# Three places of a four-layer graph network: result places behind the gate, more store buffers and numbers by GpSimd, attention's weights loaded at the far end of memory

## The chip, the cores and the metric

The kernel runs on one core of a Trainium2 chip. A core has a matrix engine (TensorE; PE in the profile, its weight loads PEld), a vector engine (VectorE, DVE), a scalar engine (ScalarE, ACT), GpSimd (POOL) and SyncE (SP). Each engine works through a queue of its own in a fixed order; they wait for each other by semaphores. Transfers are issued from the queues of SP, ACT and POOL (SPq, ACTq, POOLq where a profile speaks of the queue itself) and run on 16 DMA engines that all of them share. The metric is the device time of one execution, in microseconds.

## What is computed

The network takes 2708 nodes of 256 features and a 2708 x 2708 adjacency matrix, and runs four layers, each a graph attention and a feed-forward part, all float32. The change touches what follows the second graph layer's start: the first mixture (feed-forward part of layer 1), the attention and the second mixture (feed-forward part of layer 2). Cut to those:

```python
x = x + L1_gnn(layernorm(x), adj)
# first mixture: each node is computed by its best of 8 experts
H = gelu(layernorm(x) @ W1 + b1, approximate=False)        # 1024 wide
probs = softmax(H @ Wg + bg); assign = argmax(probs)
for e in range(8):
    out = out + where(assign == e, probs[:, e] * (H @ Wd[e] + bd[e]), 0)
x = x + out
x = x + L2_gnn(layernorm(x), adj)
# second mixture, after causal self-attention
h = rmsnorm(layernorm(x), ln1_w)
q, k, v = h @ wq.T, h @ wk.T, h @ wv.T                      # rotated, causal softmax
xa = layernorm(x) + attention(q, k, v) @ wo.T
flat = rmsnorm(xa, ln2_w)
weights = top 2 of softmax(flat @ router_w.T), made to sum to 1
for e in range(8):
    hh = silu(flat @ w1[e].T) * (flat @ w3[e].T)            # 682 wide
    out = out + weights[:, e] * (hh @ w2[e].T)
x = x + xa + out
```

## The kernel before

Nodes lie on 128 partitions, in 22 tiles of rows. A recording layer traces the program, plans the order of each engine's queue and sets the semaphores; a block `with tc.issue_after(i)` puts the instructions of it behind `i`, but only those on the engine of `i`. A buffer comes from a pool (`bufs` of them under one name), and whoever takes it waits for its last users. A pool lies at the left or, with `side="right"`, at the right end of on-chip memory; when a pool is closed its place is given to later ones, which then wait for all that used it.

**Dispatch by sorting.** `Routing` gives each choice of a node a slot in its expert's region of a DRAM table (`hs`; for the first mixture a table `fnodes` of node numbers alone). Slots are worked off in tiles of 128: the first eight tiles are the first of each expert, the others belong to an expert that is known only at run time. The usual count of such tiles is 26 in the first mixture and 47 in the second; any beyond them stand in a conditional block (`others`).

**First mixture** (`top1_ffn`). Blocks of 512 nodes go through `hidden` (L943 matmuls, gelu), `gate`, and `store`, which transposes the hidden rows back (L960), copies them out (L961, by ACT for the `late` ones) and stores them by SP in DRAM (`hidden`, L964). The last two blocks are stored after all matmuls: the first of them, eight copies, into free rooms of buffers that are no longer used (`spare`, two tiles called ft and one called ht512); the second, four copies, into `hr`, three buffers. Then the numbers of the nodes are read back: `load_first` (L1629) reads 8 rows of 128 numbers by SP, 18 more loads of one row each follow on SP (L1625), TensorE turns the 8 rows (L1049), VectorE casts them (L1050), and POOL gathers the hidden rows by them, four tiles ahead (L1061, `hr<-hidden,number`). Tiles are then transposed (L1074) and multiplied (L1110), and POOL scatters the results to DRAM (L1648).

**Second graph layer** (`gat_single`). For each of four blocks of up to 768 nodes, and each of 22 source tiles j, ACT makes e (L674), VectorE masks it (L675), TensorE accumulates (L1310). At i0 = 0, j = 3 VectorE also copies the bias (`late`, L1304), and POOL adds it to X (L1307), 22 instructions. `Weights` loads w2 at the right end by SP (L1380, L1381) behind a memset of POOL (L1378).

**Attention.** The pool `a_w` holds ln1, wv, wk and wq. It lies at the left end, where the graph layer's buffers were. POOL loads the four (L1735 and the helper `load_weight`, L93), VectorE scales the three matrices by ln1 (L1739, two instructions each), and `project(0)` normalises four tiles (f, L108), transposes them (L1759) and multiplies (pv, sc). When the last projection is done, `proj.close()` frees `a_w`, and w1 of the experts is loaded at the right end.

**Second mixture** (`experts`). For each tile s: SP loads f from `hs`, four tiles ahead, into five buffers (`fetch`); `front` transposes f (L116) and ACT copies it (ft, L1972); `hidden` multiplies by w1 and w3; ACT applies silu (L2003); `gate` multiplies the two on VectorE (L2007); `transposes` turns the result (L2014), VectorE and ACT copy it (ht, L2015 and L2016); `results` multiplies by w2 (po, L2022), ACT copies (L2026) and POOL scatters to `dys` (L1648). `place` computes, from the two last columns of f, where the result goes: three small VectorE instructions in `where` (L1638, L1641, L1642). TensorE's order is written out by hand: hidden, transposes of the tile before, hidden, results, front of the next tile but one, hidden, hidden.

Of the kernel before, what the change touches and what calls it, by code (L numbers as in the profile page):

```python
# [8 lines left out]
F32 = mybir.dt.float32  # L9
# [3 lines left out]
ALU = mybir.AluOpType  # L13
# [3 lines left out]
P = 128  # L17
# [646 lines left out]
def gat_pairs(net, e, j, i0, iw, big_p, ratio):  # L664

    nc = net.nc
    v = e[:, :iw]
    i = slice(i0, i0 + iw)
    nc.scalar.activation(v, big_p[:, i], AF.Relu, bias=net.minus_one, scale=ratio)  # L674
    return nc.vector.scalar_tensor_tensor(v, v, 1.0, net.mask[:, j, i], ALU.add, ALU.mult)  # L675
# [201 lines left out]
def top1_ffn(net, ctx):  # L877
# [4 lines left out]
    nc, tc, a, X = net.nc, net.tc, net.a, net.X  # L882
    E, HID = 8, 1024
    KC = HID // P
    with ExitStack() as inner:
# [21 lines left out]
        with tc.tile_pool(name="f1tp", bufs=2, space=PSUM) as ptp, tc.tile_pool(  # L907
            name="f1h", bufs=2, space=PSUM
        ) as ph, tc.tile_pool(name="f1g", bufs=1, space=PSUM) as pg, tc.tile_pool(
            name="f1r", bufs=2  # L910
# [38 lines left out]

            def store(its, halves, late=False, room=()):  # L950


                room = list(room)
                for k, t in enumerate(its):
                    r = rows(t)
                    for n, half in enumerate(halves):
                        hr = room.pop(0) if room else rp.tile([P, 512], F32, name="hr", bufs=3)
                        ps = pg.tile([P, 4, P], F32, name=f"hr{n}")
                        for c in range(KC // 2):
                            nc.tensor.transpose(ps[:r, c, :], half[:, c, k * P : k * P + r], net.ident)  # L960
                        (nc.scalar.copy if n or late else nc.vector.tensor_copy)(  # L961
                            hr[:r], ps[:r].rearrange("p c m -> p (c m)")
                        )
                        last = nc.sync.dma_start(rows_of[span(t), n * 512 : (n + 1) * 512], hr[:r])  # L964
                return last
# [51 lines left out]

            spare = [work.tile([P, 2, 512], F32, name="spare", tag="ft") for _ in range(2)]
            spare.append(work.tile([P, KC // 2, 512], F32, name="spare", tag="ht512", bufs=3))
            room = [t[:, k, :] for t in spare for k in range(t.shape[1])]  # L1020
            for k in kept:
                store(*k, True, room)
                room = ()
        route.finish()
        prep = ctx.enter_context(tc.tile_pool(name="g2prep", bufs=1))
        with tc.tile_pool(name="f1t", bufs=1, space=PSUM) as pt, tc.tile_pool(
# [10 lines left out]
            def load(group, at):  # L1037
                node = rowed[at : at + len(group), :]
                if group[0] == 0:
                    route.load_first(node)  # L1040
                else:
                    for k, s in enumerate(group):
                        route.load(s, node[k : k + 1, :])
# [120 lines left out]
def gat_single(net, key, head, feed, elu):  # L1164
# [7 lines left out]
    with ExitStack() as ctx:  # L1172
# [121 lines left out]
        for i0, iw in chunks(W):  # L1294
            its = tiles_of(i0, iw)
            acc = [pacc.tile([P, D + 1], F32, name="acc") for _ in its]
            for j in range(NT):
                e = work.tile([P, W], F32, name="e")
                masked = gat_pairs(net, e, j, i0, iw, big_p, ratio[:, j : j + 1])
                if bias is not None and i0 == 0 and j == 3:  # L1300

                    late = small.tile([P, D], F32, name="late", bufs=1)
                    with tc.issue_after(masked.ins):
                        nc.vector.tensor_copy(late, bias)  # L1304
                    for t in range(NT):
                        r = rows(t)
                        nc.gpsimd.tensor_tensor(X[:r, t, :], X[:r, t, :], late[:r], ALU.add)  # L1307
                for k, i in enumerate(its):
                    ri = rows(i)
                    nc.tensor.matmul(  # L1310
                        acc[k][:ri], e[:, k * P : k * P + ri], V[:, j, :], start=j == 0, stop=j == NT - 1
                    )
            for k, i in enumerate(its):
                r = rows(i)
                rd = small.tile([P, 1], F32, name="rd")
                nc.vector.reciprocal(rd[:r], acc[k][:r, D : D + 1])
                if not elu:
                    nc.vector.scalar_tensor_tensor(
                        X[:r, i, :], acc[k][:r, :D], rd[:r], X[:r, i, :], ALU.mult, ALU.add
                    )  # L1320
                    continue

                h = work.tile([P, D], F32, name="h", bufs=6)
                nc.scalar.activation(h[:r], acc[k][:r, :D], AF.Copy, scale=rd[:r])
                g = work.tile([P, D], F32, name="g")
                nc.vector.tensor_scalar(g[:r], h[:r], 0.0, None, ALU.min)
                nc.scalar.activation(g[:r], g[:r], AF.Exp)
                nc.vector.tensor_scalar(h[:r], h[:r], 0.0, -1.0, ALU.max, ALU.add)
                nc.vector.tensor_tensor(g[:r], g[:r], h[:r], ALU.add)
                nc.vector.tensor_tensor(X[:r, i, :], X[:r, i, :], g[:r], ALU.add)  # L1330
# [65 lines left out]
class Routing:  # L1396
# [216 lines left out]
    def load(self, s, f):  # L1613

        sync = self.net.nc.sync
        if s < self.E:
            self.loaded = sync.dma_start(f, self.hs[s * CAP : s * CAP + P, :])
            return

        with nullcontext() if s == self.usual else self.net.tc.issue_after(self.loaded.ins):  # L1620
            row = sync.value_load(
                self.row[0:1, s : s + 1], min_val=0, max_val=(self.E - 1) * CAP + (NT - 1) * P
            )
        rows_of = self.hs[bass.ds(row, P), :]
        self.loaded = sync.dma_start(f, rows_of.rearrange("p d -> d p") if self.choices == 1 else rows_of)  # L1625

    def load_first(self, f):

        self.loaded = self.net.nc.sync.dma_start(  # L1629
            f, self.hs.rearrange("(e c) d -> e (c d)", e=self.E)[:, :P]  # L1630
        )

    def where(self, work, s, f):

# [56 lines left out]
def attention(net, route, ln2, router, weights):  # L1691
# [11 lines left out]
    with ExitStack() as ctx:  # L1703
# [25 lines left out]
        make_upper_triangular(nc, upper)  # L1729

        proj = core.enter_context(ExitStack())
        wp = proj.enter_context(tc.tile_pool(name="a_w", bufs=1))
        pp = proj.enter_context(tc.tile_pool(name="a_p", bufs=2))
        ln1 = wp.tile([P, 2], F32, name="ln1")
        nc.gpsimd.dma_start(ln1, a["d_ln1"].rearrange("(c p) -> p c", p=P))  # L1735
        wv, wk, wq = (net.load_weight(wp, a[f"d_w{n}T"], f"w{n}") for n in "vkq")
        for w in (wv, wk, wq):
            for c in range(2):
                nc.vector.tensor_scalar(w[:, c, :], w[:, c, :], ln1[:, c : c + 1], None, ALU.mult)  # L1739
        queries, results = {}, {}  # L1740

        def project(n):
# [208 lines left out]
def experts(net, route, weights, shares):  # L1951

    nc, tc = net.nc, net.tc
    E, HID, KC, KP = weights.E, weights.HID, weights.KC, weights.KP
    HALF = HID // 2
    with ExitStack() as ctx:
# [17 lines left out]
        def place(s):  # L1974
            tos[s] = route.where(work, s, fs.pop(s))
# [28 lines left out]

        def gate(s):
            h2 = hhs[s][:, :HID].rearrange("p (q m) -> p q m", q=2)
            nc.vector.tensor_tensor(h2, h2, halves.pop((s, 1))[:, :, :HALF], ALU.mult)  # L2007

        def transposes(s):
            hh = hhs.pop(s)  # L2010
# [19 lines left out]
        def through(s0, s1):  # L2030


            for s in range(s0, min(s0 + 4, s1)):
                fetch(s)
            front(s0)
            number(s0, nullcontext())
            number(s0 + 1, nullcontext())
            for q in range(2):
                last = hidden(s0, 0, q)
            silu(s0)  # L2040
            front(s0 + 1)
            for q in range(2):
                last = hidden(s0, 1, q)
            gate(s0)
            if s0 == 0:
                route.owners()
            place(s0)
            place(s0 + 1)
            if s0 == 0:
                shares()  # L2050
            for s in range(s0, s1):
                if s + 1 == s1:
                    results(s, transposes(s))
                    break
                with tc.issue_after(last.ins):
                    last = hidden(s + 1, 0, 0)
                with tc.issue_after(last.ins):
                    ht = transposes(s)
                last = hidden(s + 1, 0, 1)
                silu(s + 1)  # L2060
                with tc.issue_after(last.ins):
                    last = results(s, ht)
                if s + 4 < s1:
                    fetch(s + 4)
                if s + 2 < s1:
                    with tc.issue_after(last.ins):
                        front(s + 2)
                        place(s + 2)
                with tc.issue_after(last.ins):
                    last = hidden(s + 1, 1, 0)  # L2070
                if s + 2 < s1:
                    number(s + 2, tc.issue_after(last.ins))
                with tc.issue_after(last.ins):
                    last = hidden(s + 1, 1, 1)
                gate(s + 1)

        through(0, route.usual)
        with route.others():
# [192 lines left out]
```

## Time and profile before

| | |
|---|---|
| runs shown | 2853.90, 2859.36, 2853.67 us; median 2853.9 |
| the profiled execution's own time | 2853.26 us |
| its span | 2851.6 us |
| mean granted TensorE clock | 0.955 |
| TensorE busy | 2625.3 us, 92% of the span |
| VectorE, ScalarE, GpSimd busy | 51%, 36%, 13% |
| first mixture, hidden layer to last scatter | about 1075 to 1344 us |
| second graph layer, matmuls L1310 | 1399.5 to 1616.0 us |
| attention | 1616 to 2126 us |
| second mixture | about 2132 to 2530 us |

A line of the costliest groups reads: source line, engine, operation, output<-inputs, partitions x elements, xcount | busy us, mean ns of one | idle us of the engine just before them, and the releaser that ended most of it. In the chain that ended last each line is start, duration, and engine, tile and line of the work; "DMA f<-hs" is a transfer that the chain waited for, "issue" is time for which the profile shows no reason. A timeline line is start, duration (of the merged group), engine, line, operation, output<-inputs, and in brackets the idle time before it and what ended that.

### The profile page before, as it was taken

Reading aid. Unit: us, or ns where it says so; the run is one execution under the profiler, and the core shown is the slowest. Engines: PE = TensorE matmul, PEld = TensorE weight load, DVE = VectorE, ACT = ScalarE, POOL = GpSimd, SP = SyncE. Lnnn points to the kernel's source line nnn. Section 1 sums busy time; section 2 is a strip of 40 time slices with the busy share of each in tenths; the row PEclk is TensorE's granted clock in tenths of the full one; section 3 lists DMA queues with packets and bytes.
Section 4 is the critical chain, followed back from the end, with each engine's and each line's share of the span. In section 5 each row is a group of like instructions: output and inputs, shape, how many; then the busy total and the mean of one; then the engine's idle time right before and its main releaser. Section 6 shows DMA issues by size and latency. Waiting matters only on the chain.

```text
span 2851.6 us, 32365 instructions
## 1 busy us (share of the span) xinstructions
PE 2625.3 (92%) x11712; PEld 1616.6 (57%) x11712; DVE 1446.4 (51%) x3086; ACT 1040.0 (36%) x1639; POOL 381.5 (13%) x470
## 2 busy tenths in 40 slices
PE   5999989799999999888999899999969999969998
PEld 4667746563333444577788533333337777757885
DVE  7753348453777765422544456464653222245555
ACT  3344433224665653311543223233322221225453
POOL 1000012100000001143300123223331111110002
PEclk9999999797999999989999999899979999989999
DMA  8899210000000003753200100002031111041001
GB/s 295 288 299 326 97 65 1 3 5 1 1 1 1 1 3 115 169 176 128 85 1 1 34 23 18 16 0 94 16 117 32 30 30 34 28 137 62 1 1 40
DMA packets 107336, 197.67 MB, mean 69 GB/s; under 512 B 8831, under 2 KB 64361, under 8 KB 104341
## 3 DMA queue, kind: packets, MB, share of 16 engines
q1 hardware_dynamic: 89178, 147.89, 16.4%
q0 software_dynamic: 14624, 43.22, 4.6%
q10 hardware_dynamic: 3374, 4.46, 0.5%
q8 instruction: 98, 1.61, 0.2%
q14 instruction: 62, 0.50, 0.1%
HBM read 135.82 MB, written 59.71 MB: 69 GB/s over the span
## 4 chain that ended last, share of the span: by engine, by line
PE 74%; DVE 9%; issue 5%; DMA 5%; ACT 3%; POOL 3%; another core or an unknown queue 0%; ACTq 0%; SPq 0%; POOLq 0%; DVEq 0%
PE acc L1310 15%; PE acc L805 8%; PE acc L284 7%; PE den L816 4%; PE po L2022 4%; PE po L1836 3%; PE sc L1817 3%; PE score L273 3%; PE pv L123 3%; PE h L1990 3%; DMA f<-hs 2%; PE h L943 2%; PE po L123 2%; PE sc L1785 2%; PE pl L123 1%
## 5 line engine op out<-in xcount | busy, mean ns | idle before, releaser
L675 DVE SCALAR_TENSOR_TENSOR e<-e,mask 128x768 f32<-128x768 f32 (+2 forms) x264 | 411.3, 1573 | 310.2 <-ACT e L674 309.9
L674 ACT ACTIVATE e<-big_p,minus_one,ratio 128x768 f32<-128x768 f32 (+2 forms) x264 | 394.9, 1513 | 368.4 <-PE acc L1310 229.7
L1310 PE MATMUL acc<-V,e 128*128 128x257 f32 (+1 forms) x1936 | 433.5, 383 | 4.5 <-DVE e L675 4.4
L1310 PEld LDWEIGHTS acc<-V,e 128*128 128x128 f32 (+1 forms) x1936 | 352.3, 186 | 85.7 <-issue 32.1
L805 PE MATMUL acc<-e,V 128*64 128x512 f32 (+1 forms) x1056 | 244.3, 551 | 4.4 <-DVE e L675 4.4
L1990 PE MATMUL h<-w,ft 128*128 (+1 forms) x752 | 233.5, 453 | 0.5 <-ACT ft L1972 0.5
L284 PE MATMUL acc<-F,e 128*128 128x257 f32 x968 | 226.3, 384 | 3.1 <-DVE e L281 2.7
L284 PEld LDWEIGHTS acc<-F,e 128*128 128x128 f32 x968 | 173.4, 185 | 67.1 <-DVE e L281 28.5
L805 PEld LDWEIGHTS acc<-e,V 128*64 128x64 f32 x1056 | 107.5, 137 | 163.8 <-issue 131.2
L1817 PE MATMUL sc<-qt,kt 64*128 64x512 f32 (+5 forms) x568 | 177.2, 576 | 4.1 <-ACT e L1830 2.4
L1830 ACT ACTIVATE e<-sc 128x1024 f32<-128x1024 f32 (+3 forms) x120 | 99.6, 859 | 188.8 <-PE sc L1817 169.4
L1990 PEld LDWEIGHTS h<-w,ft 128*128 128x128 f32 x752 | 136.1, 191 | 56.7 <-issue 1.4
L281 DVE TENSOR_TENSOR e<-e,mask 128x512 f32<-128x512 f32 (+2 forms) x132 | 80.4, 625 | 150.3 <-ACT e L275 148.7
L1842 DVE TENSOR_TENSOR sum<-sum,e 128x1024 f32<-128x1024 f32 (+4 forms) x88 | 100.1, 1138 | 77.2 <-ACT e L1830 70.0
L275 ACT ACTIVATE e<-score 128x512 f32<-128x512 f32 (+2 forms) x132 | 69.7, 544 | 179.1 <-PE score L273 152.5
L2022 PE MATMUL po<-w,ht 114*128 (+1 forms) x564 | 129.5, 379 | 0.9 <-DVE ht L2015 0.9
L1836 PE MATMUL po<-e,V 128*64 128x512 f32 (+3 forms) x480 | 111.7, 547 | 16.8 <-ACT e L1830 8.7
L816 PE MATMUL den<-e,low 128*3 128x512 f32 (+1 forms) x1056 | 123.8, 542 | 0.3 <-DVE e L675 0.3
L2022 PEld LDWEIGHTS po<-w,ht 114*128 114x128 f32 x564 | 106.7, 189 | 22.6 <-DVE ht L2015 8.2
L1638 DVE TENSOR_SCALAR second<-f,down 128x1 f32<-128x1 f32 x47 | 9.9, 213 | 213.2 <-DMA f<-hs 213.2
L1817 PEld LDWEIGHTS sc<-qt,kt 64*128 64x128 f32 (+1 forms) x568 | 60.8, 191 | 94.1 <-issue 78.0
L273 PE MATMUL score<-QK 128*128 128x512 f32 (+2 forms) x264 | 112.1, 555 | 1.2 <-ACT e L275 0.7
(618 smaller groups left out, 3510.9 us busy)
## 6 DMA issues: line engine op xcount, KB each, us to landing
row<-in_adj SPq DMA_DIRECT2D x21, 1354.0 KB
raw<-in_adjT SPq DMA_DIRECT2D x35, 768.0 KB
hs<-zero SPq DMA_DIRECT2D x8, 2838.0 KB
hidden<-hr SPq DMA_DIRECT2D x34, 256.0 KB
wd<-in_f_wd SPq DMA_DIRECT2D x8, 1024.0 KB
kept<-mask SPq DMA_DIRECT2D x21, 338.5 KB
mask<-kept SPq DMA_DIRECT2D x21, 338.5 KB
f<-hs SPq DMA_DIRECT2D x47, 129.0 KB
```

Of the source, the lines that this page charges most:

```text
L123: self.nc.tensor.matmul(out, lhsT[:, c, :], rhs[:, c, :], start=first and c == 0, stop=last and c == n - 1)
L273: nc.tensor.matmul(ps[:r, :iw], QK[:, 0, span(j)], QK[:, 1, i0 : i0 + iw], start=True, stop=True)
L284: nc.tensor.matmul(acc[k][:ri], e[:r, k * P : k * P + ri], F[:r, j, :], start=j == 0, stop=j == NT - 1)
L674: nc.scalar.activation(v, big_p[:, i], AF.Relu, bias=net.minus_one, scale=ratio)
L675: return nc.vector.scalar_tensor_tensor(v, v, 1.0, net.mask[:, j, i], ALU.add, ALU.mult)
L805: made = nc.tensor.matmul(acc[n][half, :iw], V[:, j, h, :], e[:, k, i0 : i0 + iw], start=j == 0, stop=j == NT - 1)
L816: made = nc.tensor.matmul(den[g : g + Q, :iw], low[:, j, h, Q - 1 - q : 2 * Q - 1 - q], e[:, k, i0 : i0 + iw], start=False, stop=j == NT - ...
L1310: nc.tensor.matmul(acc[k][:ri], e[:, k * P : k * P + ri], V[:, j, :], start=j == 0, stop=j == NT - 1)
L1817: nc.tensor.matmul(by_pairs(ps[:r, g])[:, :, o:], kt[b, span(j)], qt[b, :, o:iw], start=True, stop=True)
L1836: nc.tensor.matmul(by_pairs(po[b])[:, :, o:], V[:r, j, g, :], by_pairs(e[:r, g])[:, :, o:], start=j == 0, stop=j == last,)
L1990: last = nc.tensor.matmul(halves[s, n][:, q, :HALF], fts[s][:, c, :], weights.w13[n][:, es[s], c, q * HALF : (q + 1) * HALF], start=c == 0 ...
L2022: last = nc.tensor.matmul(po, ht[:KP, k, :], w2[:KP, es[s], k, :], start=k == 0, stop=k == KC - 1)
```

## The change

It has three parts.

First mixture: `store` takes a room from the list for all late copies, and the list gets four more, the tile w1 (128 x 2 x 1024), whose matmuls are over by then. So the last four copies no longer use `hr`. `load_first` is issued by POOL instead of SP, and the first row load on SP is no longer put behind it.

Attention: the pool `a_w` lies at the right end, and the scalings by ln1 are put behind `net.looped`, the masked product of the graph layer's first block at j = 3. In POOL's queue, the four loads now stand behind the memset L1378 and ahead of the bias adds L1307; before, they stood behind the graph layer, after `upper`.

Second mixture: `place(s + 2)` is traced after `gate(s + 1)` and put behind it in VectorE's queue. VectorE's queue was ht, the place of a tile some way ahead, gate; now it is ht, gate, place. The orders of TensorE and ScalarE are the same in both kernels.

```diff
             def store(its, halves, late=False, room=()):
-                room = list(room)
...
-                        hr = room.pop(0) if room else rp.tile([P, 512], F32, name="hr", bufs=3)
+                        hr = room.pop(0) if late else rp.tile([P, 512], F32, name="hr", bufs=3)
...
             spare.append(work.tile([P, KC // 2, 512], F32, name="spare", tag="ht512", bufs=3))
+            spare.append(work.tile([P, 2 * HID // 512, 512], F32, name="spare", tag="w1", bufs=1))
             room = [t[:, k, :] for t in spare for k in range(t.shape[1])]
             for k in kept:
                 store(*k, True, room)
-                room = ()
...
                 masked = gat_pairs(net, e, j, i0, iw, big_p, ratio[:, j : j + 1])
+                if i0 == 0 and j == 3:
+                    net.looped = masked
...
-        with nullcontext() if s == self.usual else self.net.tc.issue_after(self.loaded.ins):
+        with nullcontext() if s in (self.E, self.usual) else self.net.tc.issue_after(self.loaded.ins):
...
     def load_first(self, f):
-        self.loaded = self.net.nc.sync.dma_start(
-            f, self.hs.rearrange("(e c) d -> e (c d)", e=self.E)[:, :P]
-        )
+        self.net.nc.gpsimd.dma_start(f, self.hs.rearrange("(e c) d -> e (c d)", e=self.E)[:, :P])
...
-        wp = proj.enter_context(tc.tile_pool(name="a_w", bufs=1))
+        wp = proj.enter_context(tc.tile_pool(name="a_w", bufs=1, side="right"))
...
-        for w in (wv, wk, wq):
-            for c in range(2):
-                nc.vector.tensor_scalar(w[:, c, :], w[:, c, :], ln1[:, c : c + 1], None, ALU.mult)
+        with tc.issue_after(net.looped.ins):
+            for w in (wv, wk, wq):
+                for c in range(2):
+                    nc.vector.tensor_scalar(w[:, c, :], w[:, c, :], ln1[:, c : c + 1], None, ALU.mult)
...
         def gate(s):
             h2 = hhs[s][:, :HID].rearrange("p (q m) -> p q m", q=2)
-            nc.vector.tensor_tensor(h2, h2, halves.pop((s, 1))[:, :, :HALF], ALU.mult)
+            return nc.vector.tensor_tensor(h2, h2, halves.pop((s, 1))[:, :, :HALF], ALU.mult)
...
                     with tc.issue_after(last.ins):
                         front(s + 2)
-                        place(s + 2)
...
-                gate(s + 1)
+                gated = gate(s + 1)
+                if s + 2 < s1:
+
+                    with tc.issue_after(gated.ins):
+                        place(s + 2)
```

## The prediction, made before the result was known

> **What bounds the kernel now.** I read the page first: TensorE is busy 92% of the span and 74% of the chain that ended last, so a gain can only come where TensorE waits on that chain. The chain's lines and the costliest groups name one such wait at once.
>
> ```profile
> PE 74%; DVE 9%; issue 5%; DMA 5%; ACT 3%; POOL 3%; another core or an unknown queue 0%; ACTq 0%; SPq 0%; POOLq 0%; DVEq 0%
> ...
> L1638 DVE TENSOR_SCALAR second<-f,down 128x1 f32<-128x1 f32 x47 | 9.9, 213 | 213.2 <-DMA f<-hs 213.2
> ```
>
> VectorE sits 213.2 us in front of the first instruction of `where` (L1638), waiting for a tile f of the second mixture. Most of that is idle time that costs nothing, so I took the chain in order of time, in a stretch of that stage:
>
> ```profile
> 2300.64 0.23 PE tp L116 x2
> 2300.87 0.02 issue
> 2300.89 1.94 DMA f<-hs
> 2302.82 0.03 issue
> 2302.85 0.22 DVE second L1638
> ...
> 2303.49 0.88 DVE hh L2007
> ...
> 2304.41 0.87 PE pt L2014 x6
> ```
>
> The load can start only when the transposes of an older tile have freed its buffer (2300.87). It lands 1.94 us later, the place runs, and only then the gate (L2007), for which TensorE's next transposes wait. The timeline of the last tiles of the same stage is the control: there no place is left in front of the gate.
>
> ```profile
> 2489.80 0.87 DVE L2007 TENSOR_TENSOR hh<-hh,h 128x682 f32<-128x682 f32 x1 [5.64 <-PE h L1990]
> 2490.72 0.63 PEld L2014 LDWEIGHTS pt<-ident,hh 128*114 128x114 f32 x6 [0.42 <-DVE hh L2007]
> ...
> 2491.63 0.69 DVE L2015 COPY ht<-pt 114x512 f32<-114x512 f32 x1 [0.96 <-PE pt L2014]
> ```
>
> The gate starts when its matmuls end, and between its end (2490.67) and the next VectorE work (2491.63) lie 0.96 us of nothing.
>
> The same chain at the start of attention, and at the end of the first mixture's hidden layer:
>
> ```profile
> 1616.59 0.73 POOL ln L1735
> 1617.32 0.72 POOL wv L93
> 1618.03 0.72 POOL wk L93
> 1618.75 7.02 DMA wq<-in_d_wqT
> ...
> 1625.80 0.49 DVE wq L1739
> ...
> 1627.22 1.54 PE tp L1759 x6
> ```
>
> ```profile
> 1213.60 0.57 ACT L961 COPY hr<-hr 20x512 f32<-20x512 f32 x1 [4.90 <-DMA hidden<-hr]
> ...
> 1215.99 0.28 SPq L1629 DMA_DIRECT2D rowed<-fnodes  x1
> ...
> 1217.64 0.24 PE L1049 MATMUL node<-ident,rowed 8*128 8x8 f32 x1 [8.70 <-DVE fpc L1610]
> ...
> 1218.89 1.00 POOL L1061 DMA_INDIRECT hr<-hidden,number  x1 [14.72 <-DMA rowed<-fnodes]
> ```
>
> In the first, the graph layer's last matmul ends at 1616.04 and TensorE waits for weights whose loads are issued only then. In the second, one small copy waits 4.90 us for a store buffer, its store leaves at 1214.2, and the numbers are read behind it.
>
> **Second mixture: places behind the gate.** The old place was tied to a TensorE instruction, which fixes nothing in VectorE's queue; the built queue has the places of tiles 0 to 5 and half of tile 6's ahead of the first gate, and stays six tiles ahead: with five buffers, the load of tile k + 6 takes the buffer of tile k + 1, whose transposes TensorE runs just before the last matmuls of tile k. The new queue is copy ht, gate, place, every tile. TensorE's order is the same in both. Price from the starts of the ft copies (L1972, one per tile): 2198.90 to 2487.49 is 34 tiles in 288.59 us, 8.488 each. Without the wait, 2149.96 to 2198.90 is 6 tiles in 48.94 us (8.157), and 2487.49 to 2520.08 is 4 in 32.59 (8.148). I take 8.155: 34 x 8.155 = 277.27, a gain of 11.3 us. At the first gate, TensorE's matmuls end at 2144.08 (2140.47 + 3.61) and the transposes start at 2145.05; 1.44 us of places (2142.70 to 2144.14) go from in front of that gate, which then ends before TensorE does, so the 0.97 us of idle TensorE goes too. Together 12.3 us.
>
> What the moved place costs: 0.21 + 0.27 + 0.16 = 0.64 us (rows L1638, L1641, L1642) in the 0.96 us just shown, so nothing, with 0.3 us to spare. Without that cover it would be 0.64 x 46 = 29 us. Its f has landed long before, because a load now starts when the place, not only the transposes, has left the buffer: about 3 us later in the tile, lands 2 us after that, and is needed four tiles (32 us) on. SP issues nothing else in this stage; POOL's result scatter needs the place two tiles later. Bounds: 9 us (if 0.07 us a tile come back as longer semaphore chains between gate and copy) to 12.8.
>
> **Attention's weights at the far end.** Four loads move from behind the graph layer's end to POOL's queue right after its memset L1378, which runs at 1374.30 to 1376.1. POOL's next work, the bias adds L1307, starts at 1404.79 after 28.69 us of idle time, so the issues (0.73 + 3 x 0.72 = 2.9 us) push nothing. They share the DMA engines with the loads of w2 (mean share 0.47 there, at 147 GB/s); 0.9 MB at that rate is 6 us, so they land near 1386, and w2 ends some 6 us later than its 1408, with no reader before the second mixture at 2146. The six scalings, 2 x (0.29 + 0.34 + 0.48) = 2.2 us, now stand in VectorE's queue behind the fourth masked product and the copy `late`, from 1404.57. The next product starts 0.8 us late (1406.8 for 1406.00) and ends at 1407.8; TensorE wants it at 1399.46 + 4 x 2.6 = 1409.9. Cost 0; if the cover of 2 us were gone, 2.2.
>
> Gain: VectorE runs without a wait until 1618.86, then waits for wv until 1621.77. After that the new queue has eleven small instructions ahead of the first f (0.08 us apart, as at 1622.3 to 1622.8), then four f of 0.33 to 0.41 with five small ones between: 1618.86 + 0.88 + 1.8 = 1621.5 for the end of the fourth f, against 1627.97. That is 6.4; the small ones depend on each other, so I take 6.2. Bounds: 4 (each of the 16 small ones takes its full 0.16 us, and the gap to ScalarE's second root is not hidden) to 6.6. The next late thing would be rope, issued at 1617.51 and first used by kt at 1635.5; it now has the DMA engines to itself.
>
> **First mixture: buffers.** With w1's room (4 rows of 512) none of the last twelve copies waits. The last copy follows its transposes (1206.12 + 2.82 = 1208.94) and ends near 1209.5 instead of 1214.17. Its store then joins the drain of the stores ahead, the last of which has landed by 1214.20 (ACT's next instruction had waited for it), so I let it land at 1214.4 instead of 1215.9: 1.5 us, bounds 1.0 to 2.3.
>
> **First mixture: numbers by POOL.** SP's load took 1217.61 - 1215.99 = 1.62 us to TensorE. POOL's own issues of plain loads take 0.57 to 0.79 us against SP's 0.28; with the same landing that is +0.3 to +0.5. The far end is a whole gather on POOL, 4.33 us from issue to TensorE (1218.89 to 1223.22): +2.7. The 4 KB load is much nearer the plain one; I take +0.8. POOL's queue in front of it is empty (last scatter issued at 1204.2), the gathers behind it need its result anyway. SP's one-row loads move up by the same step; TensorE first wants them at 1240.1. The two parts together: -0.7, bounds -2.0 to +1.7.
>
> [...]
>
> **Sum.** 12.3 + 6.2 + 0.7 = 19.2 us. Against the profiled execution's own 2853.26 us (span 2851.6 and 1.7 around it) that is 2834.1; the median of the runs, 2853.9, lies 0.6 above it, inside their scatter. I predict 2834 us.
>
> **Rivals.**
> 1. *The wait moves to the ht copy.* If places lengthen the way from gate to copy by the 0.33 us they now cost, the 12.3 us are not gained: 2846. For it: 0.3 us of room only. Against: tiles 0 to 6 already run two of the three place instructions in that gap, at 8.157 us a tile. 7%.
> 2. *The weights arrive late in the graph layer.* If POOL's loads are served only after w2's at 1408.4, they land near 1410; 2.2 us of scaling and 0.96 of product end at 1413.2, 3.3 us after TensorE wants it: 2837. For it: one pool of DMA engines. Against: their share is 0.47. 5%.
> 3. *POOL's load is as slow as a gather*, and the store gains only 1.0: +1.7 for -0.7, 2836.5. For it: POOL's waits are long (14.72 us shown). Against: 4 KB. 10%.
> 4. *Slower: the granted clock drops in the second mixture.* TensorE would then run some 380 us without a gap. 47 tiles x 8.155 = 383 us, so the whole gain is gone once the clock there falls to 383/(383 + 19.2) = 0.95, and at 0.9 the time is 2853.3 - 19.2 + 42.6 = 2877. For it: slices of 0.7 and 0.8 occur. Against: the table by stages gives 1.00 for the tiles that already run without a gap, and the graph layer's 216.6 us of unbroken matmuls (from 1399.46) show 1.00. 3%.
> 5. *The change does nothing here*: 2853. The built queues show that it does; 2%.
>
> The forecast has the remaining 73%.
>
> **How the numbers follow.** The parts' bounds give a gain between 9 + 4 - 1.7 = 11.3 and 12.8 + 6.6 + 2.0 = 21.4: 2842 to 2832. Starts and ends of stages hold unexplained gaps that may shift (two waits of ScalarE of 2.5 us each at 1200 and 1203 have no releaser in the trace), for which I add 4 below; rival 1 and half of that shift put the upper end at 2845. So 2828 to 2845. What one can tell from no change is 0.2%, 5.7 us: the runs shown span 2853.67 to 2859.36. Faster by more than that means under 2848: the forecast, rivals 1 to 3 less a little, 0.93; within it 0.03; slower 0.04.
>
> **What would show it.** Right: ft copies 8.15 us apart through all 47 tiles, the idle time in front of L1638 no longer on the chain, the gate starting at the end of its matmuls; pv's first matmul about 6 us after the graph layer's last one instead of 12.5; the last store issued near 1209.6 and the first gather 0.7 us earlier. Wrong: tiles of 8.4 us with the copy L2015 late; an idle TensorE near 1410 with the scalings as releaser; a granted clock under 1.00 after 2146; more than 2.5 us between POOL's load and the transpose of its rows.

## The result and the profile after

Eight runs of the changed kernel: median 2836.57 us (2826.79 to 2844.65), beside 2856.10 us (2853.56 to 2861.85) in eight runs of the kernel before. The ratio is 0.9924 (95% interval 0.9904 to 0.9944): 19.5 us were gained. The profiled execution of the changed kernel is its shortest one: 2826.79 us, span 2824.9, clock 0.960. It lies 26.5 us under the profiled one of before, 7 us more than the medians do; where these 7 us come from is shown with the last experiment.

Lines of the changed kernel are shifted by one or two: the gate is L2009, the place L1637, L1640 and L1641, the ht copy L2017, the ft copy L1974, scores in attention L1819 (L1817 before).

The page of after, its chain by engine and the gate's group:

```profile
PE 79%; DVE 7%; issue 5%; ACT 4%; DMA 3%; POOL 3%; SPq 0%; ACTq 0%; POOLq 0%; DVEq 0%
...
L2009 DVE TENSOR_TENSOR hh<-hh,h 128x682 f32<-128x682 f32 x47 | 40.7, 866 | 259.5 <-PE h L1992 259.5
```

TensorE's share of the chain rose from 74% to 79% and the wait for transfers fell from 5% to 3%. VectorE's idle time in the second mixture is now in front of the gate, and ends with the gate's own matmuls; the group of L1638 with its 213.2 us is gone from the page. The timeline of after, one tile of that stage:

```profile
2300.09 0.87 DVE L2009 TENSOR_TENSOR hh<-hh,h 128x682 f32<-128x682 f32 x1 [5.64 <-PE h L1992]
2300.87 0.21 DVE L1637 TENSOR_SCALAR second<-f,down 128x1 f32<-128x1 f32 x1
...
2301.01 0.87 PE L2016 MATMUL pt<-ident,hh 128*114 128x128 f32 x6
2301.12 0.27 DVE L1640 TENSOR_SCALAR second<-second,f,dhas 128x1 f32<-128x1 f32 x1
2301.42 0.16 DVE L1641 TENSOR_TENSOR to<-second,dspare 128x1 int32<-128x1 f32 x1
...
2301.92 0.69 DVE L2017 COPY ht<-pt 114x512 f32<-114x512 f32 x1 [0.34 <-PE pt L2016]
```

The place runs in the gap between gate and ht copy and leaves 0.34 us of it. The starts of the ft copies are 8.15 to 8.17 us apart from the third tile to the last; before, 34 of them were 8.38 to 8.70.

The chain of after at the start of attention:

```profile
1611.78 2.27 PE acc L1311 x9
...
1619.71 0.81 PE tp L1761 x4
...
1621.64 3.09 PE pv L123 x16
```

The graph layer's last matmul starts at 1615.1 and pv at 1621.4: 6.4 us, where before's took 12.9 by the same measure. No load of a weight is on this stretch of the chain any more. The timeline of after, where the scalings went:

```profile
1402.82 0.96 DVE L675 SCALAR_TENSOR_TENSOR e<-e,mask 128x768 f32<-128x768 f32 x1 [2.32 <-ACT e L674]
...
1403.90 0.47 DVE L1741 TENSOR_SCALAR wv<-wv,ln 128x128 f32<-128x128 f32 x2
1404.21 8.16 POOL L1308 TENSOR_TENSOR X<-X,late 128x256 f32<-128x256 f32 x8 [25.91 <-issue]
1404.29 1.56 DVE L1741 TENSOR_SCALAR wk<-wk,ln 128x256 f32<-128x256 f32 x2
...
1405.77 1.81 DVE L1741 TENSOR_SCALAR wq<-wq,ln 128x512 f32<-128x512 f32 x2
...
1407.50 2.88 DVE L675 SCALAR_TENSOR_TENSOR e<-e,mask 128x768 f32<-128x768 f32 x2
```

The six scalings take 3.7 us (1403.90 to 1407.58), not the 2.2 of the sum. TensorE does not wait for it: from the start of this layer's first matmul to the start of its last it needs 216.2 us, as before.

The timeline of after at the end of the first mixture's hidden layer:

```profile
1202.03 1.07 ACT L959 COPY spare<-hr 20x512 f32<-20x512 f32 x2 [0.20 <-PE hr L958]
1202.31 0.90 POOL L1519 DMA_INDIRECT fnodes<-ftag,fto  x1 [0.30 <-issue]
1214.03 8.98 SPq L1626 DMA_DIRECT2D rowed<-fnodes  x8
...
1214.58 0.59 POOL L1630 DMA_DIRECT2D rowed<-fnodes  x1 [11.37 <-DMA rowed<-fnodes]
...
1216.98 0.24 PE L1048 MATMUL node<-ident,rowed 8*128 8x8 f32 x1 [14.49 <-DMA rowed<-fnodes]
...
1217.70 1.01 POOL L1060 DMA_INDIRECT hr<-hidden,number  x1 [2.53 <-DVE at L1055]
...
1222.20 1.97 PE L1073 MATMUL ht<-ident,hr 128*128 128x128 f32 x8 [4.97 <-DMA hr<-hidden,number]
```

The last copy is now done at 1203.1 instead of 1214.2, eleven microseconds earlier. Yet the first load of numbers leaves only 1.4 us earlier (1214.58 for 1215.99), and of these 1.0 us is an earlier start of the whole stretch (the last scatter of rows, L1519, starts at 1202.31 for 1203.27). The chain of after says what the numbers wait for now:

```profile
1203.19 10.51 DMA hidden<-spare
1213.74 0.03 issue
...
1213.95 0.04 SPq L1626
```

The last store is issued at 1203.19 and lands 10.51 us later, at 1213.70; SP starts on its next load 0.25 us after that. In before the last store was issued at 1214.20, landed 1.53 us later, at 1215.73, and SP's load of numbers went at 1215.99, 0.26 us after that.

### The profile page after: what moved, and what is told of

It is laid out like the page before. It is cut to its first block, busy times and chain, and to the rows that moved or that the text cites. A ratio compares the mean times of both kernels' runs of the same rounds, so it can differ in the third digit from the quotient of the medians.

```text
span 2824.9 us, 32348 instructions
## 1 busy us (share of the span) xinstructions
PE 2609.6 (92%) x11712; PEld 1614.8 (57%) x11712; DVE 1449.3 (51%) x3086; ACT 1039.5 (37%) x1639; POOL 382.1 (14%) x471
## 4 chain that ended last, share of the span: by engine, by line
PE 79%; DVE 7%; issue 5%; ACT 4%; DMA 3%; POOL 3%; SPq 0%; ACTq 0%; POOLq 0%; DVEq 0%
PE acc L1311 15%; PE acc L805 8%; PE h L1992 7%; PE acc L284 7%; PE den L816 4%; PE po L2024 4%; PE po L1838 4%; PE sc L1819 3%; PE score L273 3%; PE pv L123 3%; PE h L943 2%; PE po L123 2%; PE sc L1787 2%; PE pl L123 1%; DVE mask L198 1%
## 5 line engine op out<-in xcount | busy, mean ns | idle before, releaser
L1819 PE MATMUL sc<-qt,kt 64*128 64x512 f32 (+5 forms) x568 | 172.7, 566 | 4.1 <-ACT e L1832 2.4
L2009 DVE TENSOR_TENSOR hh<-hh,h 128x682 f32<-128x682 f32 x47 | 40.7, 866 | 259.5 <-PE h L1992 259.5
L1819 PEld LDWEIGHTS sc<-qt,kt 64*128 64x128 f32 (+1 forms) x568 | 59.7, 188 | 91.0 <-issue 75.1
```

The source lines that it names most:

```text
L1819: nc.tensor.matmul(by_pairs(ps[:r, g])[:, :, o:], kt[b, span(j)], qt[b, :, o:iw], start=True, stop=True)
```

## The experiments

The part of the program ahead of the change comes out up to 5 us apart from one profile to the next (POOL's last scatter of rows starts at 1202.31 to 1207.22), so each stage is read against a mark of its own. The table has, for each profile: the second mixture (start of the first h to start of the last po); attention's entry (start of the graph layer's last matmul to start of pv); the first mixture's turn (start of POOL's last scatter of rows to start of TensorE's first transposes of gathered rows, L1074 before); and attention (start of the first scores to start of the last).

| kernel | second mixture | entry | turn | attention |
|---|---|---|---|---|
| before | 399.8 | 12.9 | 19.95 | 459.3 |
| after | 387.5 | 6.4 | 19.89 | 452.3 |
| e1 place only | 387.5 | 12.7 | 19.56 | 463.7 |
| e2 weights only | 400.7 | 6.4 | 20.04 | 458.8 |
| e3 buffers only | 400.8 | 13.4 | 18.78 | 459.1 |
| e4 numbers by POOL only | 400.0 | 12.8 | 20.88 | 463.8 |
| e5 after, numbers by SP | 387.6 | 6.4 | 18.18 | 452.2 |
| e6 after, place ahead of gate | 387.9 | 6.4 | 19.70 | 452.2 |
| e7 after, place twice | 387.5 | 6.4 | 20.08 | 452.2 |
| e8 before, 7 buffers f | 410.3 | 13.1 | 19.92 | 452.3 |
| e9 after, place four times | 400.1 | 6.4 | 19.93 | 458.9 |
| e10 before, 7 f and 16 `to` | 400.7 | 13.3 | 20.42 | 458.8 |
| e11 after again | 387.5 | 6.4 | 19.53 | 452.2 |
| e12 the kernel of e5 again | 387.6 | 6.4 | 18.61 | 458.9 |

**e1: the places alone.** The kernel before with

```diff
                         front(s + 2)
-                        place(s + 2)
...
-                gate(s + 1)
+                gated = gate(s + 1)
+                if s + 2 < s1:
+                    with tc.issue_after(gated.ins):
+                        place(s + 2)
```

> The kernel before with the first edit alone: the places of the second mixture behind the gate. Theory: the wait for the load of f leaves VectorE's queue, all periods between ft copies come to 8.155 us as in the changed kernel, the second mixture (first h to last po) is 12.3 us shorter than before's, and nothing else moves; about 2844 us against the median of before, 2856. Rival 1 (the wait moves to the ht copy): periods of 8.4 us, 0 to 3 us gained. On the 7 us that attention was shorter in the changed kernel's profile than before's (scores from first to last 452.3 against 459.3 us): if that is a chance of the run (how long the granted clock stays near 0.5 after 1810), it comes out anywhere between here; if it belongs to the weights at the far end, this kernel has 459.

Measured: 2844.94 us against 2857.65, ratio 0.9947 (0.9929 to 0.9964), 12.7 us gained. All periods from the third tile on are 8.15 to 8.17 us, and the second mixture takes 387.5 us: this part is the whole difference of that stage. Rival 1 has fallen. Attention took 463.7 us, a third length.

**e6: which side of the gate.** The changed kernel with the place in front of the gate again, but of the same tile:

```diff
+                    with tc.issue_after(copied[0].ins):
+                        place(s + 2)
...
-                gated = gate(s + 1)
-                if s + 2 < s1:
-                    with tc.issue_after(gated.ins):
-                        place(s + 2)
+                with tc.issue_after(placed[0].ins) if s + 2 < s1 else nullcontext():
+                    gate(s + 1)
```

(`copied` and `placed` hold the ht copy and the last instruction of the place.)

> The changed kernel with each place in front of its gate (copy ht, place, gate) and of the same tile as there. Theory (what counted was that the places ran six tiles ahead, so that their loads were late, not on which side of the gate they stand): periods of 8.155 us as in the changed kernel, since VectorE sits 5.6 us in front of the gate. Rival (the side counts): the gate is late by the place's 0.64 us, periods of 8.8 us, 28 us longer.

Measured: 2826.49 us against 2855.05, ratio 0.9893 (0.9867 to 0.9919); periods of 8.16, one of 8.51. The side does not count. VectorE has nothing to do for 5 us in front of the gate, and a place whose f has landed costs nothing there. What cost time was its distance, six tiles ahead.

**e7 and e9: how much room the gap has.** The changed kernel with the place worked out twice, and four times:

```diff
                     with tc.issue_after(gated.ins):
+                        for _ in range(3):
+                            route.where(work, s + 2, fs[s + 2], "idle")
                         place(s + 2)
```

(This is e9; e7 has one call more, with the names of the place itself.)

> The changed kernel with each place worked out twice behind the gate (3 more small instructions a tile, 0.64 us, their result unused). Theory (between the place's end and the ht copy lie 0.34 us): the ht copy is 0.30 us late in every tile, po with it, periods of 8.30 to 8.45 us, 7 to 13 us longer than the changed kernel. Rival (po has other slack): periods of 8.155, no change.

> The changed kernel with each place worked out four times behind the gate; the three more have tiles of their own and no reader. Worked out twice, the six instructions took 0.89 us instead of 0.64 and left 0.15 us in front of the ht copy. Theory (room of 0.34 us): each further one adds 0.19 to 0.25, so the ht copy comes 0.2 to 0.35 us late and po with it: periods of 8.35 to 8.5 us, the second mixture 9 to 15 us longer than 387.5. Rival (there is no such limit): 8.155.

Measured: e7 2828.48 us against 2855.05 (0.9908; 0.9881 to 0.9936), periods unchanged. The six instructions overlap: they took 0.89 us from the first start to the last end, not 1.28, and so stayed inside the room; my price of 0.64 us for the second place was wrong. The timeline of e7, and then of e9, from the transposes to the ht copy:

```profile
2303.35 0.87 PE L2016 MATMUL pt<-ident,hh 128*114 128x128 f32 x6
...
2304.25 0.69 DVE L2017 COPY ht<-pt 114x512 f32<-114x512 f32 x1 [0.15 <-PE pt L2016]
```

```profile
2305.05 0.87 PE L2016 MATMUL pt<-ident,hh 128*114 128x128 f32 x6
...
2306.34 0.68 DVE L2017 COPY ht<-pt 114x512 f32<-114x512 f32 x1
...
2307.08 2.86 PE L2024 MATMUL po<-w,ht 114*128 x12
```

In e7 the copy starts 0.90 us after the transposes, as in after (0.91), and no longer waits 0.34 us but 0.15. In e9 it starts 1.29 us after them, 0.38 late, and periods rise to 8.43, by 0.275: 2847.08 us in its one run. (The last of the twelve place instructions runs behind the ht copy here.) So the room is the 0.34 us that the timeline showed, and TensorE has about 0.1 us more.

**e8 and e10: more buffers instead.** The kernel before with `name="f", bufs=7` for 5 (e8), and with `name="to", bufs=16` for 8 besides (e10).

> The kernel before with 7 buffers for f instead of 5, nothing else. Theory (a load waited for its buffer, which transposes of an older tile free): each load starts two tiles (16 us) earlier, lands long before its place, and periods are 8.155 us or a little more, 11 to 12 us gained, about 2844. Rival (the load waits for something else, SP's queue or the DMA engines): periods stay at 8.488, 2856.

> The kernel before with 7 buffers for f and 16 for `to` instead of 5 and 8. With 7 for f alone the places stand eight tiles ahead of their gate in VectorE's queue (six with 5), and wait there twice: for f, and for a `to` that a result scatter still reads. Theory (the queue runs as many tiles ahead as there are buffers, and one more, so that the last place always waits for a load that has only just been released; the `to` wait comes on top of it): without the second wait the periods are those of before, 8.45 to 8.55 us, and the second mixture lasts 400 us instead of 410. Rival (the buffers do help, and only the `to` wait hid it): 8.155 us, 387.5.

Measured: e8 2867.02 us against 2855.05, ratio 1.0038 (1.0018 to 1.0057), 12 us longer. My expectation was wrong in the sign. The timeline of e8, one tile:

```profile
2305.91 9.07 SPq L1625 DMA_DIRECT2D f<-hs  x2
...
2306.34 0.97 POOL L1648 DMA_INDIRECT dys<-y,to  x1 [4.26 <-ACT ft L1972]
2308.05 0.21 DVE L1638 TENSOR_SCALAR second<-f,down 128x1 f32<-128x1 f32 x1 [5.41 <-DMA f<-hs]
2308.30 0.27 DVE L1641 TENSOR_SCALAR second<-second,f,dhas 128x1 f32<-128x1 f32 x1
2308.78 0.16 DVE L1642 TENSOR_TENSOR to<-second,dspare 128x1 int32<-128x1 f32 x1 [0.21 <-DMA dys<-y,to]
2308.86 0.87 DVE L2007 TENSOR_TENSOR hh<-hh,h 128x682 f32<-128x682 f32 x1
```

The place still waits for a load issued 2.1 us before it. With 5 buffers for f VectorE's queue has the place six tiles ahead of the gate, with 7 eight tiles: the planner uses the added buffers to run further ahead, so the last place again stands behind a load whose buffer has only just come free. With 7 it also reaches the eighth `to`, which a result scatter issued at 2306.34 still reads (landing at 2308.76); that is the second wait, and periods are 8.74. With 16 `to` (e10) it is gone, periods are 8.42 to 8.62, and the second mixture takes 400.7 us, as before. More buffers do not help here; a fixed place in the order does.

**e2: the weights alone.** The kernel before with `side="right"` for `a_w` and the scalings behind `net.looped`, as in the change.

> The kernel before with the second edit alone: attention's weights at the far end, loaded and scaled in the graph layer. Theory: the graph layer's matmuls stay unbroken (216.6 us from first to last), pv's first matmul comes 5.4 to 6.3 us after the graph layer's last one instead of 12.7, the tiles of the second mixture stay at 8.488 us; gain 6.2 to 7.1 us, about 2849 against 2856. Rival 2 (weights late in the graph layer): an idle TensorE of some 3 us near 1410 with a scaling as releaser, gain 3. On attention's other 7 us: chance of the run, so anywhere from 452 to 459; if they belong to this edit, 452 here and not in the other three.

Measured: 2848.47 us against 2857.65, ratio 0.9964 (0.9948 to 0.998), 9.2 us; in its profile the entry takes 6.4 us, the graph layer 216.2 and the second mixture 400.7. Attention took 458.8 us here. In this one profile the shorter attention of after does not come with the weights.

**e3, e4, e5 and e12: the two parts of the first mixture.** The kernel before with the store buffers alone (e3), with `load_first` by POOL alone (e4), and the changed kernel with `load_first` by SP, in front of its row loads as before (e5, and once more as e12, beside the changed kernel on one chip):

```diff
-        self.net.nc.gpsimd.dma_start(f, self.hs.rearrange("(e c) d -> e (c d)", e=self.E)[:, :P])
+        self.loaded = self.net.nc.sync.dma_start(
+            f, self.hs.rearrange("(e c) d -> e (c d)", e=self.E)[:, :P]
+        )
```

> The kernel before with the store buffers alone; the numbers are read by SP as before. Theory (the rows are read as soon as the stores have landed, and these are set by the DMA engines' rate, not by when they were issued): the last store is issued near 1203 instead of 1214.3, yet SP's load comes only 1.0 to 2.1 us earlier than before's 1215.99, and the first gather as much before its 1218.89; about 2855. Rival (the copy that waited 4.90 us set the end): SP's load about 5 us earlier, near 1211.

> The kernel before with the first load of numbers issued by POOL alone, the store buffers as before. Theory: the step costs, from POOL's issue to TensorE's transpose 2.4 us where SP took 1.62, so the first gather comes 0.8 to 1.3 us later than before's 1218.89, and the time is 1 us longer (2857, not to be told from no change). Rival (the issue on SP stood behind the last stores, and POOL has nothing in front of it): POOL's load goes out with the last scatter's landing, 1 to 3 us earlier than 1215.99, and the first gather with it.

> The changed kernel with its first load of numbers issued by SP again, in front of SP's one-row loads. Theory: 1.62 us from the issue to TensorE instead of 2.40, and SP is released 0.55 us ahead of POOL: first gather 0.8 to 1.3 us earlier than the changed kernel's (measured from the last block's store), about 1 us less in all, near 2835.5 against the median 2836.6; in rounds not to be told from the changed kernel. Rival (the one-row loads, now behind it, come late): TensorE waits near 1240 and the gain is lost.

> The changed kernel with its first load of numbers by SP, once more beside the changed kernel on the same chip. Theory: from POOL's last scatter of rows to TensorE's first transposes of gathered rows 18.2 us against 19.7 to 20.1 of the changed kernel, and 1.5 us less in all where the clock is the same; in the medians this is at the edge of what can be told.

Measured: e3 2855.19 against 2857.65 (0.9991; 0.9976 to 1.0006), e4 2856.21 (1.0001; 0.9988 to 1.0015), e5 2833.96 against 2855.05 (0.9925; 0.9905 to 0.9945), e12 2836.18 against 2854.78 (0.9931; 0.9911 to 0.995). None of these is told from its neighbour by its time; the turn in the table tells them apart. With four buffers too few and SP it takes 19.56 to 20.42 us (five profiles, mean 19.98), with the buffers and SP 18.18 to 18.78 (three, 18.52), with the buffers and POOL 19.53 to 20.08 (five, 19.83), with POOL alone 20.88. By these means the buffers bring 1.5 us, and POOL's load takes 1.3 of them back. The timeline of e5 has SP's load:

```profile
1217.07 0.32 SPq L1630 DMA_DIRECT2D rowed<-fnodes  x1
...
1218.93 0.24 PE L1048 MATMUL node<-ident,rowed 8*128 8x8 f32 x1 [6.94 <-DMA rowed<-fnodes]
```

From SP's issue to the transpose 1.86 us (1.65 to 1.86 in all profiles with SP), from POOL's 2.35 to 2.58; and POOL issues 0.55 us behind SP where both wait for the same end (1214.58 and 1214.03 in after). Further on it blurs. From the same scatter to the second graph layer's first matmul the four kinds take 196.0 to 199.3, 194.3 to 196.7, 195.3 to 196.6 and 197.1 us: the rival (one-row loads late, the graph layer later) did not show, but 1.3 us are not told apart there either. In e3 the rival (5 us earlier once the copy no longer waits) has fallen too: SP's load left at 1216.86, not near 1211.

What sets the moment of the load is the landing of the last store of hidden rows. In all 14 profiles the first numbers leave just behind it: SP starts on its first load 0.25 to 0.27 us after it (0.48 in e4), and POOL's load leaves 0.87 or 0.88 us after it, with the semaphore of that store among those it waits for. The scatters that wrote the numbers had landed before, by 0.2 us in after and by 1.4 to 3.2 us in the others. Where the last store is issued late (before, e1, e2, e4, e8, e10) it lands 1.5 us after its issue; where it is issued early it lands 4.2 to 10.5 us after, among the other stores. Its distance from the last scatter's start tells what the buffers brought: its issue lies 10.3 to 11.3 us behind that start without them and 0.9 to 6.7 with them, its landing 11.9 to 12.9 (mean 12.4) and 10.5 to 11.6 (mean 11.2). On average the store leaves 5.6 us earlier and lands 1.2 us earlier; this is what the theory of e3 said.

Counted from that landing to TensorE's first transposes, the two ways of loading are told apart without overlap: 7.39 to 7.70 us with SP (eight profiles, mean 7.57), 8.37 to 8.50 with POOL (six, mean 8.43). POOL's load costs 0.9 us. The other 0.4 of the 1.3 lies ahead of the landing, where the kernels with POOL's load and those with SP's do the same work.

Why a load that reads `fnodes` waits for stores to `hidden` was not tried. A reason may be its buffer: `rowed` comes from a pool that is opened when the pools of the stored rows are closed, and such a pool waits for all that used its place. If so, another place for `rowed` would let the load leave with the scatters.

**e11: the changed kernel again.**

> The changed kernel once more, beside the next one. Theory (attention's length is a chance of the run: 452, 459 or 464 us between the first and the last scores by how long the granted clock stays at 0.5 after the stop at 170 us): one of these three lengths, and a median of 2832 to 2838 against 2855 of before. If 452 belongs to the changed kernel, 452 again and a median near 2827.

Measured: 2837.81 us against 2854.78, ratio 0.9935 (0.9912 to 0.9958), six runs from 2823.89 to 2841.59; in the profile attention took 452.2 us. Over all 14 profiles the length of attention is one of three: 452 in six, 459 in six, 464 in two. The same kernel has 452.2 as e5 and 458.9 as e12; e8 has 452.3 with nothing of the change. The table by windows of before and of after, at the same place of attention (168 us after its first scores; columns: length, busy us and instructions of TensorE, its weight loads, VectorE, ScalarE, POOL, then the granted clock, DMA share, GB/s):

```profile
1810.00:1820.00 10.00, 7.62 (x27) 3.60 (x28) 7.40 (x28) 2.60 (x4) 5.28 (x4) 0.79 0.07 25
1820.00:1830.00 10.00, 9.07 (x21) 2.44 (x20) 1.20 (x3) 1.02 (x1) 6.03 (x7) 0.50 0.24 83
1830.00:1840.00 10.00, 10.00 (x18) 2.34 (x17) 5.47 (x5) 1.58 (x2) 0.00 (x0) 0.50 0.00 0
1840.00:1850.00 10.00, 10.00 (x39) 3.85 (x38) 2.45 (x2) 3.66 (x4) 0.00 (x0) 0.84 0.00 1
```

```profile
1803.00:1813.00 10.00, 7.62 (x27) 3.43 (x24) 7.44 (x28) 2.60 (x4) 5.60 (x4) 0.77 0.08 27
1813.00:1823.00 10.00, 8.80 (x26) 2.38 (x24) 2.11 (x2) 1.02 (x1) 5.71 (x7) 0.72 0.23 81
1823.00:1833.00 10.00, 9.69 (x38) 2.98 (x34) 5.48 (x6) 4.03 (x5) 0.00 (x0) 1.00 0.00 0
```

TensorE is idle for 2.4 us of the first window in both, and the clock there is 0.79 and 0.77. In after it is back at 1.00 in the third window; in before it stays at 0.50 through 1840 although TensorE is busy for 19.1 of these 20 us, and the 18 matmuls of the third window fill it. Those are the 7 us of the profiles that no part of the change explains. Why a profile gets the short or the long drop is open: of the seven profiles of the changed kernel and its variants (after, e5, e6, e7, e9, e11, e12) five have the short one, of the seven built on before one, which is too few to say that the change has no hand in it. The medians carry it too: e6 and e7 lie 8 to 10 us under the changed kernel's, with the same work or more and the same stages in their profiles.

## Why the prediction was right

The forecast was 2834 us and 19.2 gained; measured 2836.6 and 19.5. That the two gains agree to 0.3 us is in part luck: the interval of the ratio allows 16 to 27 us, and attention alone differs by 7 us between two profiles of one kernel (e5 and e12). What bears the forecast out is the steps, each read against its own mark:

- **Places behind the gate, 12.3 us**: 12.3 in the two profiles (399.8 to 387.5), 12.7 as the mean over the table (400.3 for before, e2, e3 and e4; 387.6 for those with the new place and no added work). The tile of 8.155 us and the 0.97 at the first gate (8.87 to 7.78 us between the second and third ft copies) came as read. The step's reason was right as well: e6, e8 and e10 show that it is the six tiles, set by the buffers, that made the gate wait for a load.
- **Room of 0.3 us behind the gate**: 0.34, and e9 shows what lies behind it.
- **Attention's weights, 6.2 us**: 6.6 (12.93 to 6.37). Mis-sized was the cost in the graph layer that was set at nothing: 3.7 us of scalings instead of 2.2. The next masked product (1.48 us from 1407.50) ended at 1409.0 and TensorE wanted it at 1409.3 (1398.88 + 4 x 2.6), so of the cover of 2 us 0.3 was left. The durations had been taken with POOL idle, where wk and wq took 0.34 and 0.48 us each (before, 1623.05 to 1626.76); in after POOL's adds (L1308) run at the same time, from 1404.21 on, and they took 0.82 and 0.95. Whether the adds are the cause was not shown: no run here has the scalings beside an idle POOL at that place.
- **Store buffers, 1.5 us**: 1.2 (the last store's landing, over all profiles), 1.1 in the two profiles of before and after. The picture was right: the late store held the numbers back (they leave 0.26 us after it has landed), and once issued early it joins the drain of the stores ahead. The prediction expected it out at 1209.6; in after it left at 1203.19, since ScalarE's two unexplained waits did not occur there, and landed with the others all the same.
- **Numbers by POOL, +0.8 us**: 0.9, from the landing to TensorE's transposes. Its make-up differs from the sum: the load leaves 0.6 us later after the landing (0.88 for 0.26) and takes some 0.7 us longer to TensorE (2.35 to 2.58 for 1.65 to 1.86), but POOL's first gather then starts 0.72 us after that instead of 1.25. By these ranges the loads' durations alone differ by 0.5 to 0.9.

Together the first mixture's turn brought 0.15 us by the means of the table and 0.06 in the two profiles, instead of 0.7, and the three parts come to 12.7 + 6.6 + 0.15, or 19.4. Rival 3 (a load as slow as a gather, +1.7, and 1.0 from the store) gave a loss of 0.7: the store came near its figure, the load did not. Rivals 1, 2 and 5 are refuted by e1, the unbroken graph layer and the periods. Rival 4 did not occur where it was placed: the periods stay at 8.155 through 44 tiles, with a granted clock of 1.00 from 2146 to 2510 us in after. What moved with the granted clock was attention, by 7 us in one and the same kernel (after the same stop the clock is 0.68, 0.80 and 1.00 over three windows of 10 us in e5, and 0.67, 0.67, 0.50 and 0.79 over four in e12). Over all profiles its length differs by up to 11.6 us; the prediction took its scatter from three runs and had no term for this. It is larger than two of the three parts of the change, and a range around a sum from one profile should hold it.

Undoing the one part that costs (numbers by SP again, e5 and e12) gives a kernel that is 1.3 us shorter in the turn than the changed one, 0.9 of it from the load itself, with medians of 2833.96 and 2836.18 us beside 2836.57 and 2837.81. The turn shows the gain; neither the times nor the graph layer's start do.

## What to carry to other kernels

An instruction that is not needed yet, but stands in an in-order queue ahead of one that is, makes the queue wait for its data (here places six tiles ahead of the gate: 12.7 us in e1); look for idle time in front of a tiny instruction, and fix its place behind the urgent one. If a planner fills the queue as far ahead as buffers allow, more buffers can move the wait and add others (seven f for five in e8: 12 us longer). Where two changes meet at one point, measure them apart on a mark near by: here one took back most of what the other gave, and only distances between neighbouring events showed it. Issuing a store earlier helped here only until it met the stores ahead of it: it left 5.6 us earlier on average and landed 1.2 us earlier.

## What the runs showed of the hardware

- In attention of before, TensorE was idle for 2.4 us of 10 (1810 to 1820); the granted clock was 0.79 in that window, 0.50 from 1820 to 1840 with TensorE busy for 19.1 of the 20 us, 0.84 from 1840 to 1850 and 1.00 from 1850 to 1860. In after, with the same 2.4 us idle (1803 to 1813), it was 0.77, then 0.72, and 1.00 from 1823 to 1833.
- The small instructions of VectorE on 128x1 of two independent places overlap: in e7 two chains of three took 0.89 us from the first start to the last end (2303.21 to 2304.10), in after one took 0.71 (2300.87 to 2301.58), so the second cost 0.2 us.
- The 4 KB load of numbers took 2.35 to 2.58 us from its issue to TensorE in the six profiles where POOL issued it, 1.65 to 1.86 in the eight where SP did; POOL's left 0.87 to 0.88 us after the landing of the last store, and SP started on its first load 0.25 to 0.27 us after it (0.48 in e4).
